# A four-layer graph network: an LSTM written with Tanh alone, and other ranks for the last units and blocks

## The chip, the cores and the metric

The kernel runs on one core of a Trainium2 chip. The core has a matrix engine (TensorE, "PE" in the profile; its weight loads are "PEld"), a vector engine (VectorE, "DVE"), an engine for activation functions and scaled copies (ScalarE, "ACT"), a general engine (GpSimd, "POOL") and a queue for transfers (SyncE, "SP"). Each works through its own instructions in order and waits on semaphores for the others. Matmul results go to PSUM, everything else lies in SBUF. The metric is device time in microseconds (us) from the first to the last instruction and the little that lies around it.

## The reference

The input x has 128 graphs of 64 nodes with 256 features, in float32. Four layers follow each other, each `x = layernorm(x + layer(x, adj))`.

- Layer 0: aggregation with the normalised adjacency, 256 to 512 features, batch norm, ReLU, back to 256, batch norm.
- Layer 1: a Chebyshev step (it needs the largest eigenvalue of adj), layer norm, attention with 4 heads (softmax, so Exp), layer norm, an MLP with Gelu, layer norm.
- Layer 2: two graph convolutions, and then four LSTMs in turn over windows of p = 1, 2, 3 and 4 nodes, where the last hidden state of a window replaces its last node:

```python
def step(carry, x_t):
    h, c = carry
    g = x_t @ Wih.T + h @ Whh.T + bias
    i, f, gg, o = jnp.split(g, 4, axis=-1)
    c = jax.nn.sigmoid(f) * c + jax.nn.sigmoid(i) * jnp.tanh(gg)
    h = jax.nn.sigmoid(o) * jnp.tanh(c)
    return ((h, c), None)
```

- Layer 3: graph attention: a product with W, scores, softmax over neighbours (Exp), the weighted sum, and two layer norms around it.

The change uses that sigmoid(z) = (tanh(z/2) + 1) / 2.

## The kernel before

The work is cut into 16 blocks of 8 graphs (512 rows of 256 features). Layer 0 runs as a stage of its own. Then a second call of `flow` lays out everything else. `flow` is a planner that runs while the program is built: each task is a generator that yields its steps with an engine, a planned duration and what it needs (`step(e, us, ps, sl, ..., at, tbl)`: PSUM tiles, SBUF slots, a time at which its inputs are due, the activation table). The planner always takes, of all running tasks, the step that could start first, and the instructions of all engines are issued in that order. A margin per engine (`MARGIN`, line 30; line 177) is added to the time at which a step's input is due before steps are compared, so that a step with a fresh input stands behind one whose input has long been there. Among equals the smaller rank wins. Nothing of this runs on the chip: there, each engine follows the order written.

Tasks come in streams with a width (how many run at once) and a rank (lines 1677 to 1690):

- `end` (rank 2, width 4): layer 3 for the blocks 12 to 15 in halves, 8 tasks of `last_block`
- `gcn` (rank 3, width 2): layer 2's graph convolutions and the LSTM with p = 1, by block
- `seq` (rank 4, width 6): the end of layer 0 and layer 1, by block
- `units` (rank 5, width 2): the LSTMs with p = 2, 3, 4 in 16 units, all but the last three
- the last three units (rank 1.5, width 1, "urgent", which means without margin): p = 4 for the third group of graphs, and for the fourth in two halves
- `last` (rank 6, width 4): layer 3 for the blocks 0 to 11.

An LSTM unit (`lstm`, line 1025) takes up to 512 windows. The first step has no h: it needs the gates i, g and o (lines 1055 for the products, 1067 for the activations), i times g on POOL (line 1086), Tanh of the cell (line 1094) and o times that on DVE (line 1102, or an `out_of` that writes the result into the state). Later steps of a large unit use a Strassen scheme with seven products in place of eight (line 1127 for the matmuls; stages 1 to 4 evict and combine on ACT and DVE, lines 1165 to 1195; activations at 1203 to 1207, i times g on POOL at 1220, the cell on DVE at 1228 and 1231, Tanh at 1236, h at 1243). The units with half the graphs use `plain_steps` (line 1250): products at 1264 and 1266, activations at 1269, i times g on POOL at 1280, the cell at 1282 and 1284, Tanh at 1286, h at 1296. Writing to the state is at lines 1357 (p = 1) and 1389.

A block of layer 3 (`last_block`, line 1456): x is fetched by SP, h is copied on ACT (1467), turned on PE (359), added (1478) and normed (lines 272 to 274 on DVE, 308 on POOL, 311 on DVE, 314 on ACT). Then it is turned again (353, copies at 1492 and 1494), multiplied by W (1507, 1517, 1519), scored (1527, 1531, 1532, 1536 to 1540), put through Exp (1544), divided (1546, 1547), turned (1553, 1555), multiplied (1563), added (1574), normed and stored. In layer 1 Exp is at line 854 and Gelu at line 928. Before an activation whose function isn't in the table that ACT holds, the program has a load of a table.

Of the kernel before, what the change touches and what calls it, by code (L numbers as in the profile page):

```python
# [26 lines left out]
BG = B // NG  # L27
EPS = 1e-5
LAG, LAG_T = 0.06, 0.2
MARGIN = {"T": 2.0, "V": 0.5, "S": 0.5}  # L30


@with_exitstack
def kernel(ctx: ExitStack, tc: tile.TileContext, a: dict, out: bass.AP):
# [23 lines left out]
    class Clock:  # L58
        end = 0.0
# [914 lines left out]
    bl = load_col(gw, "bih", a["L2_gnn_bih"])  # L974
    bh = load_col(gw, "bhh", a["L2_gnn_bhh"])
    V.tensor_tensor(bl, bl, bh, ALU.add)

    def gcn_rows():

# [45 lines left out]
    def lstm(p, n, parts, x_of, out_of):  # L1025

        us = n * 1.68e-3
        v_us, g_us, s_us = (0.05 + n * r for r in (1.25e-3, 2.3e-3, 1.15e-3))  # L1030

        def bias(g, c):
            return bl[:, p - 1, 2 * g + c : 2 * g + c + 1]

        def of(sl):
            return mem[sl][:, : 2 * n].rearrange("p (c k) -> p c k", c=2)
# [25 lines left out]
            return t, ps, sl  # L1062

        def gates(pair, t, ps, sl):
            t = yield step("S", 0.1 + n * 2.5e-3, ps=-1, at=t, waits=False, tbl="sigmoid")
            for j, (g, c) in enumerate(pair):
                S.activation(of(sl)[:, j], fm(PS[ps])[:, j, :n], AF.Tanh if g == 2 else AF.Sigmoid, bias=bias(g, c))  # L1067
            PS.give(ps)
            return t, sl

# [10 lines left out]
        for c in range(2):  # L1081
            if c:
                tb, sb = yield from gates(((0, 1), (2, 1)), *other)
            t, sl = (tb, sb) if c else (ta, sa)
            t = yield step("G", g_us, at=t, waits=False)
            G.tensor_tensor(of(s_cell)[:, c], of(sl)[:, 0], of(sl)[:, 1], ALU.mult)
            tc_.append(t)
        t_o, s_o = yield from gates(((3, 0), (3, 1)), *to)
        s_h = None
        for c in range(2):  # L1090
            sl = (sa, sb)[c]
            th = of(sl)[:, 1]
            t = yield step("S", s_us, at=tc_[c], waits=False, tbl="sigmoid")
            S.activation(th, of(s_cell)[:, c], AF.Tanh)
            o = of(s_o)[:, c]
            t = yield step("V", v_us, at=max(t, t_o), sl=0 if p == 1 or c else 1, waits=False)
            if p == 1:
                last_h(c, o, th)
            else:
                if c == 0:  # L1100
                    s_h = mem.take()
                V.tensor_tensor(of(s_h)[:, c], o, th, ALU.mult)
            mem.give(sl)
            h_at = t
        mem.give(s_o)

        if len(parts) == 1 and p > 1:
            yield from plain_steps(p, n, us, of, bias, x_of, lambda ap: spread(ap, 0), last_h, s_cell, s_h, h_at)
            return


# [24 lines left out]
        for s in range(1, p):  # L1136
# [59 lines left out]

            def stage4(g):
                v, y = places(g)
                f = AF.Tanh if g == 2 else AF.Sigmoid
                t = yield step("T", us, at=max(t_h[2], at[g]), waits=False)  # L1200
                product(g, "A22", T4, v[:, 0, :])
                yield step("S", 0.1 + n * 1.15e-3, at=at[g, "0"], waits=False, tbl="sigmoid")
                S.activation(of(act[g])[:, 0], of(act[g])[:, 0], f, bias=bias(g, 0))  # L1203
                yield step("S", copy_us, at=at[g], waits=False, tbl="sigmoid")
                S.activation(y[:, 3, :], y[:, 3, :], f, bias=bias(g, 1))
                at[g] = yield step("S", copy_us, ps=-1, at=t, waits=False, tbl="sigmoid")
                S.activation(y[:, 2, :], v[:, 0, :], f, bias=bias(g, 1))
                PS.give(tiles[g])

            yield from stage1(0)  # L1210
# [5 lines left out]
            yield from stage4(0)  # L1216
            yield from stage1(1)
            yield from stage4(2)
            t_g = yield step("G", 2 * g_us, at=at[2], waits=False)
            G.tensor_tensor(of(act[2]), of(act[0]), of(act[2]), ALU.mult)  # L1220
            mem.give(act[0])
            yield from stage1(3)
            for stage in (stage2, stage3):
# [1 line left out]
                yield from stage(3)  # L1225
            yield from stage4(1)
            yield step("V", 2 * v_us, at=at[1], waits=False)
            V.tensor_tensor(cell, cell, of(act[1]), ALU.mult)
            mem.give(act[1])
            t = yield step("V", 2 * v_us, at=t_g, waits=False)  # L1230
            V.tensor_tensor(cell, cell, of(act[2]), ALU.add)
            yield from stage4(3)
            for j in held:
                mem.give(j)
            t = yield step("S", 2 * s_us, at=t, waits=False, tbl="sigmoid")
            S.activation(of(act[2]), cell, AF.Tanh)
            t = yield step("V", 2 * v_us, at=max(t, at[3]), sl=0 if last else 1, waits=False)
            if last:
                for c in range(2):
                    last_h(c, of(act[3])[:, c], of(act[2])[:, c])  # L1240
            else:
                s_h = mem.take()
                V.tensor_tensor(of(s_h), of(act[3]), of(act[2]), ALU.mult)
# [6 lines left out]
    def plain_steps(p, n, us, of, bias, x_of, shaped, last_h, s_cell, s_h, h_at):  # L1250

        v_us, g_us, s_us = (0.05 + n * r for r in (1.25e-3, 2.3e-3, 1.15e-3))
        for s in range(1, p):
            last = s == p - 1
            x = x_of(s, 0)

            def products(pair):
                t = yield step("T", 8 * us, ps=1, sl=1, at=h_at - 2 * us, waits=False)
                ps, sl = PS.take(), mem.take()
                for j, (g, c) in enumerate(pair):  # L1260
                    m = slice(g * D + c * P, g * D + (c + 1) * P)
                    dst = fm(PS[ps])[:, j, :n]
# [4 lines left out]
                t = yield step("S", 0.3 + n * 2.1e-3, ps=-1, at=t, waits=False, tbl="sigmoid")  # L1267
                for j, (g, c) in enumerate(pair):
                    S.activation(of(sl)[:, j], fm(PS[ps])[:, j, :n], AF.Tanh if g == 2 else AF.Sigmoid, bias=bias(g, c))
                PS.give(ps)  # L1270
                return t, sl

            ends = []
            for c in range(2):
                cell = of(s_cell)[:, c]
                ta, sa = yield from products(((0, c), (2, c)))
                tb, sb = yield from products(((1, c), (3, c)))
                A, F = of(sa), of(sb)
                tg = yield step("G", g_us, at=ta, waits=False)
                G.tensor_tensor(A[:, 1], A[:, 0], A[:, 1], ALU.mult)  # L1280
                t = yield step("V", v_us, at=tb, waits=False)
                V.tensor_tensor(cell, cell, F[:, 0], ALU.mult)
                t = yield step("V", v_us, at=max(t, tg), waits=False)
                V.tensor_tensor(cell, cell, A[:, 1], ALU.add)
                t = yield step("S", s_us, at=t, waits=False, tbl="sigmoid")
                S.activation(A[:, 1], cell, AF.Tanh)
                ends.append((c, t, sa, sb))

            for c, t, sa, sb in ends:
                t = yield step("V", v_us, at=t, sl=0 if last or c else 1, waits=False)  # L1290
                if last:
                    last_h(c, of(sb)[:, 1], of(sa)[:, 1])
                else:
                    if c == 0:
                        h_new = mem.take()
                    V.tensor_tensor(of(h_new)[:, c], of(sb)[:, 1], of(sa)[:, 1], ALU.mult)
                mem.give(sa)
                mem.give(sb)
            mem.give(s_h)
            if not last:  # L1300
                s_h = h_new
            h_at = t
        yield step("V", 0.0, at=h_at, waits=False)
        mem.give(s_cell)

    def gcn_block(i):
# [47 lines left out]


        def out_of(q, c, o, th):
            V.tensor_tensor(
                hT_block(i)[:, c, :, :].rearrange("p n b -> p b n"), o, th, ALU.mult
            )

        yield step("T", 0.0)
# [6 lines left out]
    def unit(p, g, w0, nw, b0, nb):  # L1368
# [17 lines left out]
            return half(src[:, :, :, s, :], q)  # L1386

        def out_of(q, c, o, th):
            V.tensor_tensor(half(src[:, c, :, p - 1, :], q), o, th, ALU.mult)

        yield from lstm(p, nw * nb, parts, x_of, out_of)
        mark("p", p, g, w0, nw, b0, nb)
# [63 lines left out]
    def last_block(i, t0=0, nt=NT):  # L1456
# [18 lines left out]
        mem.give(s_h)  # L1475
        mark("read", i)
        yield step("V", 0.1 + 1.2 * r, ps=-1)
        V.tensor_tensor(x, px, x, ALU.add)
        PS.give(ps)
        yield from ln_steps_act(x)  # L1480

# [189 lines left out]
    def last_of(i, *part):  # L1671
# [67 lines left out]
```

## Time and profile before

| | us |
|---|---|
| median of 3 runs | 2408.22 (2407.28 to 2410.26) |
| profiled execution | 2409.44 |
| its span | 2407.7 |
| busy: PE / DVE / ACT / POOL | 2287.2 / 1287.7 / 1187.4 / 591.7 |
| mean granted PE clock | 0.982 |

The profile is of one execution. Busy times are sums over the span; the clock is a share of full speed. A line such as "L1086 POOL ... x12 | 15.3, 1276" names a line of the kernel, the engine, the operation, the count, the summed time in us and the mean time of one in ns; what follows is how long the engine stood idle before them and for whom it waited. The DVE line of the page, in 40 slices of the span, shows where that engine is busiest:

```profile
DVE  4557678566483474744643433454444444455546
ACT  2257643544434544335453443444444653468766
```

Layer 1 runs to about slice 20, the LSTM units from there to slice 37, layer 3 beside the last of them and after.

### The profile page before, as it was taken

The page shows a single profiled execution, that of the slowest core. Times are in us where ns is not written, and L with a number is a line of the kernel's source. Part 1 is how long each engine was busy: PE and PEld are TensorE (multiplying, and loading weights), DVE is VectorE, ACT ScalarE, POOL GpSimd, SP SyncE. Part 2 cuts the span into 40 slices and gives each one's busy share as a digit, 9 for nine tenths or more (in the row PEclk, how much of TensorE's full clock was granted, in tenths as well). Part 3 has the DMA queues.
Part 4 walks back from the last instruction along what each step waited for, and adds up shares of the span by engine and source line. Part 5 has one row for each costly group of instructions (what it writes and reads, how often), then busy time and mean ns, then how long its engine had stood idle before and what let it go on. Part 6 is the DMA issues. An engine that isn't in the chain of part 4 may idle for free.

```text
span 2407.7 us, 40603 instructions
## 1 busy us (share of the span) xinstructions
PE 2287.2 (95%) x16916; PEld 1759.9 (73%) x16916; DVE 1287.7 (53%) x2904; ACT 1187.4 (49%) x2189; POOL 591.7 (25%) x441
## 2 busy tenths in 40 slices
PE   8999788999989999999999999999999999998997
PEld 4548665666665666666667788899999888887785
DVE  4557678566483474744643433454444444455546
ACT  2257643544434544335453443444444653468766
POOL 0012134232242232331321222222221222122122
PEclk9999899999999999999999999999999999999998
DMA  6100301000000000001000000000001000001111
GB/s 162 49 1 1 111 23 49 28 10 10 1 12 17 10 10 10 1 10 36 36 19 27 18 1 1 17 2 1 1 1 36 1 10 9 19 27 66 40 36 45
DMA packets 42633, 57.91 MB, mean 24 GB/s; under 512 B 6224, under 2 KB 35536, under 8 KB 42448
## 3 DMA queue, kind: packets, MB, share of 16 engines
q1 hardware_dynamic: 41344, 54.22, 7.0%
q8 instruction: 133, 2.18, 0.4%
q10 hardware_dynamic: 1104, 1.08, 0.1%
q14 instruction: 52, 0.43, 0.1%
HBM read 38.52 MB, written 16.78 MB: 23 GB/s over the span
## 4 chain that ended last, share of the span: by engine, by line
PE 60%; DVE 16%; ACT 7%; POOL 3%; issue 2%; POOLq 0%; ACTq 0%; DVEq 0%
PE ps L1127 26%; PE ps L1055 11%; PE ps L365 7%; PE ps L377 4%; PE ps L938 4%; DVE ln_st L272 3%; ACT x L314 2%; PE ps L808 2%; POOL ln_rs L308 1%; PE ps L1507 1%; DVE x L300 1%; PE ps L341 1%; DVE ln_mv L273 1%; PE ps L353 1%; DVE ln_nm L311 1%
## 5 line engine op out<-in xcount | busy, mean ns | idle before, releaser
L1127 PE MATMUL ps<-x,x 128*128 128x256 f32 x928 | 225.0, 380 | 0.7 <-DVE t L1195 0.7
L1127 PEld LDWEIGHTS ps<-x,x 128*128 128x128 f32 x928 | 173.5, 190 | 24.9 <-issue 1.6
L314 ACT ACTIVATE x<-x,ln_nm,ln_rs 128x256 f32<-128x256 f32 x212 | 112.3, 592 | 133.3 <-DVE ln_nm L311 131.9
L1127 PE MATMUL ps<-t,x 128*128 128x256 f32 x672 | 163.7, 380 | 0.0
L1127 PEld LDWEIGHTS ps<-t,x 128*128 128x128 f32 x672 | 126.4, 190 | 17.1 <-DVE x L1195 0.8
L308 POOL TENSOR_TENSOR ln_rs<-ln_rs,neghalf 128x4 f32<-128x4 f32 (+1 forms) x72 | 71.2, 990 | 212.0 <-DVE ln_rs L274 186.4
L365 PE MATMUL ps<-t,W1T 128*128 128x512 f32 x256 | 117.8, 607 | 0.0
L1055 PE MATMUL ps<-h,wL 128*128 128x192 f32 (+2 forms) x480 | 103.9, 371 | 4.8 <-ACT h L1353 4.8
L272 DVE BATCH_NORM_STATS2 ln_st<-x 128x6 f32<-128x256 f32 x260 | 99.7, 403 | 0.4
L1055 PEld LDWEIGHTS ps<-h,wL 128*128 128x128 f32 x480 | 75.6, 192 | 29.9 <-issue 22.5
L294 POOL TENSOR_TENSOR ln_rs<-ln_rs,neghalf 128x4 f32<-128x4 f32 x32 | 36.9, 1153 | 217.1 <-DVE ln_rs L274 217.0
L1055 PE MATMUL ps<-h,x 128*128 128x256 f32 x384 | 86.7, 380 | 2.2 <-ACT t L1067 1.8
L1067 ACT ACTIVATE t<-ps,bih 128x512 f32<-128x512 f32 (+3 forms) x98 | 57.2, 634 | 55.8 <-PE ps L1055 55.1
L1203 ACT ACTIVATE x<-x,bih 128x512 f32<-128x512 f32 (+2 forms) x69 | 44.6, 648 | 80.3 <-DVE x L1193 80.0
L1186 DVE COPY x<-ps 128x256 f32<-128x256 f32 (+2 forms) x69 | 26.1, 378 | 108.4 <-PE ps L1127 107.6
L365 PEld LDWEIGHTS ps<-t,W1T 128*128 128x128 f32 x256 | 47.6, 195 | 49.6 <-issue 49.5
L365 PE MATMUL ps<-t,wA 128*128 128x512 f32 x160 | 76.8, 626 | 5.5 <-ACT t L784 5.5
L1055 PEld LDWEIGHTS ps<-h,x 128*128 128x128 f32 x384 | 72.6, 190 | 12.9 <-ACT t L1067 2.2
L1186 DVE COPY t<-ps 128x256 f32<-128x256 f32 (+2 forms) x51 | 18.8, 373 | 103.8 <-PE ps L1127 103.5
L1067 ACT ACTIVATE x<-ps,bih 128x512 f32<-128x512 f32 (+3 forms) x86 | 51.5, 650 | 40.6 <-PE ps L1055 40.4
L273 DVE BATCH_NORM_AGGREGATE ln_mv<-ln_st 128x2 f32<-128x6 f32 x448 | 71.3, 167 | 0.0
L1193 DVE TENSOR_TENSOR x<-ps,x 128x512 f32<-128x512 f32 (+2 forms) x69 | 41.4, 602 | 53.0 <-PE ps L1127 43.6
(714 smaller groups left out, 5713.2 us busy)
## 6 DMA issues: line engine op xcount, KB each, us to landing
t<-in_x_dram SPq DMA_DIRECT2D x26, 512.0 KB, 4.3
xd<-x SPq DMA_DIRECT2D x16, 512.0 KB, 2.6
x<-xd SPq DMA_DIRECT2D x8, 512.0 KB, 3.3
out_dram<-x SPq DMA_DIRECT2D x8, 512.0 KB, 2.9
h<-in_x_dram SPq DMA_DIRECT2D x5, 512.0 KB, 5.2
wL<-in_L_gnn_Wih_dram SPq DMA_DIRECT2D x2, 1024.0 KB, 5.0
x<-in_L_gnn_Whh_dram SPq DMA_DIRECT2D x2, 1024.0 KB, 5.4
x<-xd SPq DMA_DIRECT2D x5, 256.0 KB, 2.9
```

The source lines that it names most:

```text
L272: V.bn_stats(st[:, t, :], y[:, t, :])
L273: V.bn_aggr(mv[:, t, :], st[:, t, :])
L308: G.tensor_tensor(rs, rs, neghalf[:, :n], ALU.pow)
L314: S.activation(y[:, t, :], y[:, t, :], AF.Identity, scale=rs[:, t : t + 1], bias=nm[:, t : t + 1])
L365: T.matmul(ps[:, c, :], w[:, k, (off + c) * P : (off + c + 1) * P], yT[:, k, :], start=(k == 0), stop=(k == nk - 1),)
L377: T.matmul(ps[:, t, :], yT[:, k, t * P : (t + 1) * P], w[:, k, :], start=(k == 0), stop=(k == nk - 1),)
L808: T.matmul(pv[r * N : (r + 1) * N, b, :, :], x1T[:, k, b * N : (b + 1) * N], Wv_par[:, k, r, :, :], start=(k == 0), stop=(k == 1),)
L938: T.matmul(tm(PS[ps])[:, t, :], fm(mem[gs[k // 2]])[:, k % 2, t * P : (t + 1) * P], W2[:, k, :], start=(k == 0), stop=(k == 3),)
L1055: T.matmul(spread(fm(PS[ps])[:, j, :n], q), WL[p][0][:, k, m], x_of(0, q)[:, k], start=(k == 0), stop=(k == 1),)
L1067: S.activation(of(sl)[:, j], fm(PS[ps])[:, j, :n], AF.Tanh if g == 2 else AF.Sigmoid, bias=bias(g, c))
L1127: T.matmul(dst, WS[p][name](k, g), y[:, k], start=first and k == 0, stop=k == 1, skip_group_check=not first)
L1186: V.tensor_copy(y[:, 1, :], v[:, 0, :])
```

## The change

All gates use Tanh. A gate that was sigmoid(z) is now tanh(z/2), and what multiplies it adds one: (tanh(z/2) + 1) times y is twice sigmoid(z) times y. So the cell and h are kept doubled. A helper `gate` scales the product by 0.5 (0.25 for a sigmoid gate of a p above 1, whose inputs are doubled themselves), the biases of i, f and o are halved once, and layer 3 halves h when it adds it to x. Inputs of the LSTM with p = 1 aren't doubled.

i times g goes from POOL to DVE (`times`, a scalar_tensor_tensor). The planned steps of the LSTM no longer name an activation table.

In the planner, the margin for PE goes from 2.0 to 0.5, the last three units join the stream `units` (rank 5, width 2, with margin), and `end` goes from rank 2 to 5.5.

```diff
-MARGIN = {"T": 2.0, "V": 0.5, "S": 0.5}
+MARGIN = {"T": 0.5, "V": 0.5, "S": 0.5}
...
     V.tensor_tensor(bl, bl, bh, ALU.add)
+    for j in (slice(0, 4), slice(6, 8)):
+        V.tensor_scalar(bl[:, :, j], bl[:, :, j], 0.5, None, ALU.mult)
...
-        def bias(g, c):
-            return bl[:, p - 1, 2 * g + c : 2 * g + c + 1]
+        def gate(dst, z, g, c):
+            S.activation(
+                dst,
+                z,
+                AF.Tanh,
+                bias=bl[:, p - 1, 2 * g + c : 2 * g + c + 1],
+                scale=(1.0 if g == 2 else 0.5) * (1.0 if p == 1 else 0.5),
+            )
+
+        def times(dst, y, z):
+
+            V.scalar_tensor_tensor(dst, y, 1.0, z, ALU.add, ALU.mult)
...
-            t = yield step("S", 0.1 + n * 2.5e-3, ps=-1, at=t, waits=False, tbl="sigmoid")
+            t = yield step("S", 0.1 + n * 2.5e-3, ps=-1, at=t, waits=False)
             for j, (g, c) in enumerate(pair):
-                S.activation(of(sl)[:, j], fm(PS[ps])[:, j, :n], AF.Tanh if g == 2 else AF.Sigmoid, bias=bias(g, c))
+                gate(of(sl)[:, j], fm(PS[ps])[:, j, :n], g, c)
...
-            t = yield step("G", g_us, at=t, waits=False)
-            G.tensor_tensor(of(s_cell)[:, c], of(sl)[:, 0], of(sl)[:, 1], ALU.mult)
+            t = yield step("V", v_us, at=t, waits=False)
+            times(of(s_cell)[:, c], of(sl)[:, 0], of(sl)[:, 1])
...
-            S.activation(th, of(s_cell)[:, c], AF.Tanh)
+            t = yield step("S", s_us, at=tc_[c], waits=False)
+            S.activation(th, of(s_cell)[:, c], AF.Tanh, scale=0.5)
...
-                V.tensor_tensor(of(s_h)[:, c], o, th, ALU.mult)
+                times(of(s_h)[:, c], o, th)
...
-                S.activation(of(act[g])[:, 0], of(act[g])[:, 0], f, bias=bias(g, 0))
+                gate(of(act[g])[:, 0], of(act[g])[:, 0], g, 0)
...
-            t_g = yield step("G", 2 * g_us, at=at[2], waits=False)
-            G.tensor_tensor(of(act[2]), of(act[0]), of(act[2]), ALU.mult)
+            t_g = yield step("V", 2 * v_us, at=at[2], waits=False)
+            times(of(act[2]), of(act[0]), of(act[2]))
...
-            V.tensor_tensor(cell, cell, of(act[1]), ALU.mult)
+            times(cell, of(act[1]), cell)
...
-            V.tensor_tensor(cell, cell, of(act[2]), ALU.add)
+            V.scalar_tensor_tensor(cell, cell, 0.5, of(act[2]), ALU.mult, ALU.add)
...
-                G.tensor_tensor(A[:, 1], A[:, 0], A[:, 1], ALU.mult)
+                tg = yield step("V", v_us, at=ta, waits=False)
+                times(A[:, 1], A[:, 0], A[:, 1])
...
-            V.tensor_tensor(half(src[:, c, :, p - 1, :], q), o, th, ALU.mult)
+            V.scalar_tensor_tensor(half(src[:, c, :, p - 1, :], q), o, 1.0, th, ALU.add, ALU.mult)
...
-        V.tensor_tensor(x, px, x, ALU.add)
+        V.scalar_tensor_tensor(x, px, 0.5, x, ALU.mult, ALU.add)
...
-            Stream(4, 2, end),
+            Stream(4, 5.5, end),
             Stream(2, 3, gcn),
             Stream(6, 4, seq),
-            Stream(2, 5, units[:-3]),
-            Stream(1, 1.5, units[-3:], urgent=True),
+            Stream(2, 5, units),
             Stream(4, 6, last),
```

The remaining lines do the same at the other places of the LSTM (the Tanh of the cell, the later steps of both schemes, the write of p = 1).

More of the change, by code (lines that the diff above doesn't have):

```diff
@@ L1092, in lstm @@
             th = of(sl)[:, 1]
-            t = yield step("S", s_us, at=tc_[c], waits=False, tbl="sigmoid")
-            S.activation(th, of(s_cell)[:, c], AF.Tanh)
+            t = yield step("S", s_us, at=tc_[c], waits=False)
+            S.activation(th, of(s_cell)[:, c], AF.Tanh, scale=0.5)
             o = of(s_o)[:, c]
@@ L1107, in lstm @@
         if len(parts) == 1 and p > 1:
-            yield from plain_steps(p, n, us, of, bias, x_of, lambda ap: spread(ap, 0), last_h, s_cell, s_h, h_at)
+            yield from plain_steps(p, n, us, of, gate, times, x_of, lambda ap: spread(ap, 0), last_h, s_cell, s_h, h_at)
             return
@@ L1198, in stage4 @@
                 v, y = places(g)
-                f = AF.Tanh if g == 2 else AF.Sigmoid
                 t = yield step("T", us, at=max(t_h[2], at[g]), waits=False)
                 product(g, "A22", T4, v[:, 0, :])
[L1202 to L1207, printed above, removed]
+                yield step("S", 0.1 + n * 1.15e-3, at=at[g, "0"], waits=False)
+                gate(of(act[g])[:, 0], of(act[g])[:, 0], g, 0)
+                yield step("S", copy_us, at=at[g], waits=False)
+                gate(y[:, 3, :], y[:, 3, :], g, 1)
+                at[g] = yield step("S", copy_us, ps=-1, at=t, waits=False)
+                gate(y[:, 2, :], v[:, 0, :], g, 1)
                 PS.give(tiles[g])
@@ L1234, in lstm @@
                 mem.give(j)
-            t = yield step("S", 2 * s_us, at=t, waits=False, tbl="sigmoid")
-            S.activation(of(act[2]), cell, AF.Tanh)
+            t = yield step("S", 2 * s_us, at=t, waits=False)
+            S.activation(of(act[2]), cell, AF.Tanh, scale=0.5)
             t = yield step("V", 2 * v_us, at=max(t, at[3]), sl=0 if last else 1, waits=False)
@@ L1242, in lstm @@
                 s_h = mem.take()
-                V.tensor_tensor(of(s_h), of(act[3]), of(act[2]), ALU.mult)
+                times(of(s_h), of(act[3]), of(act[2]))
             mem.give(act[3])
@@ L1248, in lstm, with plain_steps @@
         mem.give(s_cell)
-    def plain_steps(p, n, us, of, bias, x_of, shaped, last_h, s_cell, s_h, h_at):
+    def plain_steps(p, n, us, of, gate, times, x_of, shaped, last_h, s_cell, s_h, h_at):
         v_us, g_us, s_us = (0.05 + n * r for r in (1.25e-3, 2.3e-3, 1.15e-3))
@@ L1266, in products @@
                         T.matmul(dst, WL[p][1][:, k, m], of(s_h)[:, k], start=False, stop=(k == 1))
-                t = yield step("S", 0.3 + n * 2.1e-3, ps=-1, at=t, waits=False, tbl="sigmoid")
+                t = yield step("S", 0.3 + n * 2.1e-3, ps=-1, at=t, waits=False)
                 for j, (g, c) in enumerate(pair):
-                    S.activation(of(sl)[:, j], fm(PS[ps])[:, j, :n], AF.Tanh if g == 2 else AF.Sigmoid, bias=bias(g, c))
+                    gate(of(sl)[:, j], fm(PS[ps])[:, j, :n], g, c)
                 PS.give(ps)
@@ L1278, in plain_steps @@
                 A, F = of(sa), of(sb)
-                tg = yield step("G", g_us, at=ta, waits=False)
-                G.tensor_tensor(A[:, 1], A[:, 0], A[:, 1], ALU.mult)
+                tg = yield step("V", v_us, at=ta, waits=False)
+                times(A[:, 1], A[:, 0], A[:, 1])
                 t = yield step("V", v_us, at=tb, waits=False)
-                V.tensor_tensor(cell, cell, F[:, 0], ALU.mult)
+                times(cell, F[:, 0], cell)
                 t = yield step("V", v_us, at=max(t, tg), waits=False)
-                V.tensor_tensor(cell, cell, A[:, 1], ALU.add)
-                t = yield step("S", s_us, at=t, waits=False, tbl="sigmoid")
-                S.activation(A[:, 1], cell, AF.Tanh)
+                V.scalar_tensor_tensor(cell, cell, 0.5, A[:, 1], ALU.mult, ALU.add)
+                t = yield step("S", s_us, at=t, waits=False)
+                S.activation(A[:, 1], cell, AF.Tanh, scale=0.5)
                 ends.append((c, t, sa, sb))
@@ L1295, in plain_steps @@
                         h_new = mem.take()
-                    V.tensor_tensor(of(h_new)[:, c], of(sb)[:, 1], of(sa)[:, 1], ALU.mult)
+                    times(of(h_new)[:, c], of(sb)[:, 1], of(sa)[:, 1])
                 mem.give(sa)
@@ L1356, in out_of @@
         def out_of(q, c, o, th):
-            V.tensor_tensor(
-                hT_block(i)[:, c, :, :].rearrange("p n b -> p b n"), o, th, ALU.mult
+            V.scalar_tensor_tensor(
+                hT_block(i)[:, c, :, :].rearrange("p n b -> p b n"), o, 1.0, th, ALU.add, ALU.mult
             )
```

## The prediction

> **What bounds the kernel now.** I read the page first, then one table by stage, then what holds TensorE up in the stages that lose time.
>
> ```profile
> PE 2287.2 (95%) x16916; PEld 1759.9 (73%) x16916; DVE 1287.7 (53%) x2904; ACT 1187.4 (49%) x2189; POOL 591.7 (25%) x441
> ...
> PEclk9999899999999999999999999999999999999998
> ```
>
> Matmuls fill 95% of the span; no other engine passes 53%. The change neither adds nor removes a matmul (8,844 in the program of either kernel), so it can only act on the 120.5 us in which TensorE stands still and on the slower clock after such gaps. Where these lie, from the windows view (length; then busy time of PE, PEld, DVE, ACT and POOL; then granted clock, DMA share, GB/s):
>
> ```profile
> 0.00:300.00 300.00, 266.51 (x2004) 178.37 (x2005) 174.33 (x363) 148.14 (x250) 31.01 (x41) 0.95 0.22 65
> 300.00:1260.00 960.00, 912.15 (x8578) 609.04 (x8577) 576.39 (x1246) 432.70 (x560) 306.98 (x186) 0.98 0.05 18
> 1260.00:2100.00 840.00, 834.57 (x4550) 743.09 (x4549) 369.67 (x719) 382.90 (x853) 188.61 (x136) 1.00 0.03 10
> 2100.00:2369.20 269.20, 252.09 (x1630) 213.31 (x1629) 144.84 (x477) 196.94 (x458) 56.62 (x66) 0.99 0.12 41
> 2369.20:2407.70 38.50, 21.84 (x161) 16.12 (x160) 22.50 (x101) 26.72 (x71) 8.53 (x14) 0.82 0.15 49
> ```
>
> PE idle by row: 33.5 (layer 0, before the first difference in the order), 47.9 (layer 1 and layer 2's graph part), 5.4 (the LSTM stage), 17.1 (the last LSTM units beside layer 3), 16.7 (the tail after the last LSTM matmul). The LSTM stage, which most of the edits touch, runs PE at 99.4%: nothing is to be had there. The other rows decide. What ACT does in them, by groups of instructions:
>
> ```profile
> L928 ACT ACT_TABLE_LOAD x18 | 23.1, 1283 | 3.2 <-issue 2.3 <-PE ps L365 0.6
> ...
> L1067 ACT ACT_TABLE_LOAD x17 | 21.8, 1283 | 33.9 <-PE ps L1055 33.7
> ...
> L1544 ACT ACT_TABLE_LOAD x16 | 20.5, 1283 | 5.5 <-DVE mx L1540 5.3
> ...
> L854 ACT ACT_TABLE_LOAD x13 | 16.7, 1283 | 13.3 <-DVE h L852 9.5 <-DVE t L852 3.6
> ```
>
> With fifteen more (ten at line 1269, five at lines 1203, 1205 and 584) there are 79 loads, 1.28 us each, because Sigmoid, Exp and Gelu sit in different tables. On the chain of waits (start, length, what) between 2150 and 2300 thirteen of them stand, for example:
>
> ```profile
> 2158.49 1.28 ACT L1544
> ...
> 2161.24 1.28 ACT L1203
> ```
>
> PE's own waits from 2100 on are spread over many small ones, behind ACT, DVE and POOL alike:
>
> ```profile
> PE ps L353 <- ACT x L314: 2.9, 1, 2.9
> PE ps L1563 <- ACT h L1555: 2.8, 1, 2.8
> PE ps L1553 <- ACT t L1207: 2.5, 1, 2.5
> ```
>
> [...] The order of the changed kernel agrees: 19 loads are left, eight for Exp and nine for Gelu in layer 1, one at line 584 and one for Exp later; none stands at an LSTM line, so Tanh also runs from the table that Gelu loaded. [...] at 2161.24 the load begins 20 ns after the instruction before it ended, and the next starts 10 ns after the load. I use 1.28. [...] line 1228 on 128x768 takes 0.95 us in most instances and 2.56 in one, line 1231 on 128x1024 takes 1.22 in most groups and 1.55 on average in another. [...] in the tail row above the clock is 0.82.
>
> **The change part by part.**
>
> *Tanh for Sigmoid.* The activations keep number and shape; a constant factor in place of none is not shown as a price of its own, and I take zero. 60 loads go: 60 x 1.283 = 77 us less ACT work. Beside a full PE most of this is worth nothing. On the path it can return what stood on the chain: 13 x 1.28 = 16.7 us at 2150 to 2300, and four loads (at 480.9, 489.7, 1140.4 and 1225.0) = 5.1 us in layers 1 and 2. It can't return more than PE was idle (17.1 us in the fourth row), and once a load is gone the next wait is a layer norm's (DVE statistics, POOL power, ACT scaling). I take 11 and 4; bounds 3 to 17 and 0 to 20 (the upper end if the 40 us of loads freed in layers 1 and 2 also shorten other blocks' chains).
>
> *Products with "+1" on DVE.* 119 multiplications leave POOL (lines 1086, 1220, 1280: 87 + 67 + 9 = 163 us) and come to DVE as scalar_tensor_tensor. Row by row such an instruction costs what a tensor_tensor does (line 1538: 420 ns, line 1547: 423 ns, both 128x256), so DVE gains 74 x about 0.6 + 33 x about 1.05 + 12 x 0.42 = 84 us, mostly in the LSTM stage, where it is 44% busy. A link of the chain falls from 1.27 to 0.69 us (128x512), under a full PE: zero. Queued behind them on DVE are the evictions of the Strassen products; 84 us in 840 more raise DVE to 54%, which I price at zero to +3. With 163 us less of POOL [...] I take -2 (bounds -6 to 0). The halved biases are two small instructions (line 274's kind, 0.26 us each) beside layer 1: zero. Line 1478's addition becomes one that also halves, at the same price.
>
> *Ranks and streams.* The last three LSTM units join the common stream of two, and layer 3's last half blocks fall behind the LSTM. In the changed order 6.5 of layer 3's 16 blocks end after the last LSTM matmul (four whole ones and five halves); before it was 2.5. So the tail grows and what lies before it shrinks. A whole block costs PE, from the timeline at full clock, 0.87 + 0.87 (transposes) + 3.65 (Wx) + 0.86 (scores) + 0.6 + 1.03 = 7.9 us. What is issued after the last LSTM matmul sums to 48 us of PE (17 before), 60 of ACT (before: 26.7 by the same count, and the window shows 26.72), 63 of DVE (28 by the same count, where the window shows 22.5 because short instructions overlap, so about 50). ACT decides. Between 2160 and 2220 ACT reached 90%, in the old tail 69%. At 85% the tail takes 60/0.85 + 4 for the last copies and store = 74 us. Of it 26 are not PE work; in the old tail 38.5 - 17 = 21.5 were not. Cost: +4; bounds -4 (95%) to +15 (69%).
> The order of SP's loads moves with it: x of blocks 14 and 15 is fetched late, behind a store that waits for its block, yet 2.6 us per fetch lie beside 4 us of that block's own copies: zero to +3.
>
> *PE margin 2.0 to 0.5.* It changes the order nearly everywhere from layer 1 on: a product may now be placed when its input is due 0.5 us ahead instead of 2. Against that, older blocks go first and free their buffers. The number of changes from task to task on PE is the same (999 and 998). The trace can't price this. From below: -12, a quarter of the 47.9 us. From above: PE waited about 30 times in layers 1 and 2, some 1.6 us each; half as many again with a slower clock after some is +25. I take zero.
>
> Sum: -11 - 4 - 2 + 4 = -13. The profiled execution took 2409.4 (span 2407.7), so 2396.4; the median shown is 1.2 below that execution, so 2395.2. I say 2396.
>
> **The rivals.**
> 1. The tail decides (slower). Layer 3's last blocks are the only work left, each a chain of ACT, DVE, POOL and PE. If ACT reaches only 60% of it, the tail takes about 100 us, 52 of them not PE work: +30. Less 17 of gains: 2422. It decides from a tail of 48 + 21.5 + 17 = 87 us on. For it: the old tail reached 69% with few blocks. Against: eight blocks may run at once now.
> 2. The margin's stalls eat the gain: +16 in layers 1 and 2, 2412. For it: PE's waits are many and short. Against: in the LSTM stage, where products follow each other densely, PE waits 5 us in 840.
> 3. More comes back in layers 1 and 2: of 47.9 us idle and 2% of clock over 960 us (19 us) a third returns, 22 in place of 4: 2378.
> 4. The loads were covered and layer norm holds PE as before: the gains shrink to about 4, the tail takes 4: 2409.
>
> **How the numbers follow.** Forecast 0.40 (own range 2384 to 2406), rival 1 0.18, rival 2 0.17, rival 3 0.15, rival 4 0.10. Within 0.2% (what a measurement can tell from no change) is 2403.4 to 2413.0. Faster: 0.85 of the forecast, rival 3, a tenth of rival 2: 0.51. Same: 0.12 of the forecast, 0.6 of rival 4, 0.35 of rival 2: 0.17. Slower: 0.32. Eight times in ten: 2375 to 2424.
>
> **What would show it.** In the new profile: 19 loads, ACT near 1110 us, DVE near 1370, POOL near 430, PE unchanged near 2287 and 99% busy in the LSTM stage. From the last LSTM matmul to the end 65 to 84 us, ACT its busiest engine; PE idle before that below 8 us over a stretch like the old fourth row; PE idle from 300 to 1260 near 44. I am wrong if the tail exceeds 87 us, if the idle time in layers 1 and 2 grows by 10 us or more, or if the LSTM stage falls below 98%.

## The result and the profile after

The changed kernel takes 2440.07 us (median of four runs, 2439.28 to 2441.58), against 2407.75 us for the kernel before on the same chip: a ratio of 1.0133 with a 95% interval of 1.0115 to 1.0150. It is 1.3% slower, where the prediction said 0.5% faster. The profiled execution has a span of 2437.5 us, 29.8 more than before.

The head of the page after (busy time and share of the span by engine, number of instructions, and the granted clock in 40 slices):

```profile
PE 2294.5 (94%) x16916; PEld 1768.3 (73%) x16916; DVE 1325.7 (54%) x3025; ACT 1113.4 (46%) x2129; POOL 431.7 (18%) x322
...
PEclk9999899999989999999999999999999999999997
```

The matmuls are the same 16916 records, yet they took 7.3 us longer; the other engines moved as their instructions did. The loss has to lie in the time in which TensorE stood still and in its clock, so the windows view is read next. Its columns are length; busy time of PE, PEld, DVE, ACT, POOL; granted clock, DMA share, GB/s. The fourth row ends with the last LSTM matmul, as it did in the prediction.

```profile
0.00:300.00 300.00, 266.18 (x2005) 178.36 (x2006) 174.89 (x365) 148.36 (x250) 31.32 (x41) 0.95 0.23 65
300.00:1260.00 960.00, 891.78 (x8338) 599.65 (x8337) 559.09 (x1254) 383.78 (x515) 259.57 (x151) 0.97 0.05 17
1260.00:2080.00 820.00, 812.09 (x4636) 716.27 (x4636) 400.40 (x796) 381.22 (x847) 90.45 (x72) 1.00 0.03 12
2080.00:2350.10 270.10, 264.13 (x1511) 228.86 (x1510) 136.68 (x389) 144.03 (x363) 31.53 (x34) 0.99 0.09 29
2350.10:2437.50 87.40, 60.30 (x433) 45.14 (x431) 54.65 (x226) 55.98 (x156) 18.82 (x25) 0.81 0.15 49
```

Length less PE's busy time is the time that TensorE stood still. Against the same stages before:

| stage | idle before | idle after | |
|---|---|---|---|
| layer 0 (0 to 300) | 33.5 | 33.8 | +0.3 |
| layers 1 and 2 (300 to 1260) | 47.9 | 68.2 | +20.3 |
| LSTM (1260 to 2080) | 5.4 | 7.9 | +2.5 |
| to the last LSTM matmul | 17.1 | 6.0 | -11.1 |
| tail | 16.7 | 27.1 | +10.4 |
| PE busy over all | 2287.2 | 2294.5 | +7.3 |

The tail grew from 38.5 to 87.4 us, and that is what the eye falls on. But the long tail holds 60.3 us of PE work, where the old one held 21.8. Its idle time grew by 10.4, and that of the stage before shrank by 11.1: together nothing. The loss is layers 1 and 2, and the slower clock. Who PE waited for there, from the view of waits between 300 and 1260 us (in total, times, longest):

```profile
PE ps L341 <- ACT t L1343: 6.3, 1, 6.3
PE ps L938 <- ACT x L928: 6.1, 1, 6.1
PE ps L1071 <- ACT t L1368: 5.7, 1, 5.7
PE ps L365 <- ACT t L784: 5.5, 1, 5.5
PE ps L938 <- DVE t L898: 5.5, 1, 5.5
```

Two of these, the fourth and fifth, are there before as well. The first three are new, and each is one long stall. In this stretch after has eight single stalls of 3.3 us or more, 40 us together, where before has five, 24 us: 16 of the 20.3 us are long stalls. The third can be followed through the timeline of after (start, length, engine, line, operation, count, and in brackets the idle time before it):

```profile
524.65 0.46 DVE L297 SCALAR_TENSOR_TENSOR h<-h,ln_mv,rows 128x256 f32<-128x256 f32 x1
...
526.86 0.88 DVE L300 SCALAR_TENSOR_TENSOR h<-h,ln_rs,rows 128x256 f32<-128x256 f32 x2
527.66 5.07 DVE L297 SCALAR_TENSOR_TENSOR h<-h,ln_mv,rows 128x256 f32<-128x256 f32 x2
...
536.54 2.33 DVE L274 TENSOR_SCALAR ln_rs<-ln_mv 128x4 f32<-128x4 f32 x1
...
542.14 1.28 DVE L1360 TENSOR_TENSOR t<-ps,rb 128x512 f32<-128x512 f32 x2
...
527.40 2.55 POOL L915 TENSOR_TENSOR h<-h,rows 128x1024 f32<-128x1024 f32 x1 [0.58 <-PE ps L353]
530.03 2.41 POOL L916 TENSOR_TENSOR h<-h,rows 128x1024 f32<-128x1024 f32 x1
...
536.23 2.61 POOL L933 TENSOR_TENSOR x<-x,rows 128x1024 f32<-128x1024 f32 x1 [3.79 <-DVE h L776]
...
543.52 1.06 ACT L1368 ACTIVATE t<-t 128x1024 f32<-128x1024 f32 x1 [13.81 <-DVE t L1360]
...
535.31 3.62 PE L377 MATMUL ps<-wA,t 128*128 128x256 f32 x16
544.62 13.38 PE L1071 MATMUL ps<-t,wL 128*128 128x512 f32 x24 [5.70 <-ACT t L1368]
...
713.16 2.29 DVE L311 SCALAR_TENSOR_TENSOR ln_nm<-ln_mv,ln_rs 128x4 f32<-128x4 f32 x1 [1.12 <-POOL ln_rs L308]
...
713.10 2.34 POOL L915 TENSOR_TENSOR t<-t,rows 128x1024 f32<-128x1024 f32 x1
715.49 2.07 ACT L314 ACTIVATE x<-x,ln_nm,ln_rs 128x256 f32<-128x256 f32 x4 [11.11 <-DVE ln_nm L311]
...
719.70 1.05 ACT L1343 ACTIVATE t<-t 128x1024 f32<-128x1024 f32 x1
```

One DVE instruction of line 297 takes 0.46 us, and the next two take 5.07 together, beside two of POOL's. Line 274, 0.26 us on average before, takes 2.33 beside POOL's third. That is 4.15 + 2.07 = 6.2 us of delay, which the DVE queue hands on to line 1360, from there to the Relu on ACT at 1368, and so to the product at 1071 behind which PE's whole queue stands. Over the whole trace of after 62 DVE instructions took at least 0.5 us more than the median of their line and shape, and each of the 62 overlaps an instruction of POOL; in before it is 90 of 90. But 503 of the 3025 DVE instructions of after overlap one, so that most of these keep their time. Lines 297 and 311 read two tensors, line 274 reads one, and all three have stretched instances; what sets the stretched ones apart, the traces don't show.

The last four lines belong to the 6.3 us stall. DVE's small line 311 takes as long as POOL's line 915 beside it, some 2 us more than its usual 0.16. ACT's line 314 waits for it, and behind 314 in ACT's queue stands line 1343, for which PE waits. So the stretched instruction accounts for some 2 of the 6.3 us, and the rest is work that was queued ahead. The 6.1 us stall has no such pair: ACT's line 928 stands behind line 314, which had waited 13.12 us for a layer norm.

Such stretched instructions are not new in the changed kernel. Line 285, another part of a layer norm, has them before (first line) and after (second; count, then shortest, median and longest in ns):

```profile
L285 DVE TENSOR_SCALAR t<-t,ln_mv,ln_rs x40: 375/408/2532, 352.2 to 1224.6; 128x256 f32<-128x256 f32 x40
L285 DVE TENSOR_SCALAR t<-t,ln_mv,ln_rs x36: 374/407/2428, 354.8 to 1187.1; 128x256 f32<-128x256 f32 x36
```

Counted over all DVE instructions that took at least 0.5 us more than the median of their line and shape, the excess in layers 1 and 2 is 87 us before and 62 after. There is less of it, then, and yet PE stood still for longer: the amount of stretching doesn't explain the loss.

Such a stall costs twice. The 24 products behind this one took 13.38 us. The same 24, with no stall ahead of them, in the timeline of before:

```profile
551.18 10.46 PE L1055 MATMUL ps<-t,wL 128*128 128x512 f32 x24
```

The windows view of after shows the clock behind the stall (the 0.50 and the 1.00):

```profile
543.60:550.30 6.70, 5.67 (x7) 2.52 (x8) 5.73 (x16) 2.13 (x3) 3.47 (x2) 0.50 0.01 2
550.40:557.90 7.50, 7.50 (x19) 3.29 (x18) 5.62 (x8) 3.16 (x5) 2.34 (x1) 1.00 0.00 0
```

PE worked for 5.67 us at half its clock, and half of that, 2.8 us, is nearly all of the 2.9 us that the products took longer. So a stall of 5.7 us cost 2.9 more in the work that followed. It is not alone in this: in the trace of after PE stands still for 4.2 us or more between two matmuls 11 times, and in the 2 us behind each of these stalls the clock is 0.50.

### The profile page after: what moved, and what is told of

It is laid out like the page before. It is cut to its first block, busy times and chain, and to the rows that moved or that the text cites. A ratio compares the mean times of both kernels' runs of the same rounds, so it can differ in the third digit from the quotient of the medians.

```text
span 2437.5 us, 40485 instructions
## 1 busy us (share of the span) xinstructions
PE 2294.5 (94%) x16916; PEld 1768.3 (73%) x16916; DVE 1325.7 (54%) x3025; ACT 1113.4 (46%) x2129; POOL 431.7 (18%) x322
## 4 chain that ended last, share of the span: by engine, by line
PE 50%; DVE 11%; ACT 4%; issue 2%; POOL 1%; POOLq 0%; ACTq 0%; DVEq 0%
PE ps L1143 24%; PE ps L1071 10%; PE ps L365 5%; PE ps L938 2%; DVE ln_st L272 2%; PE ps L1522 2%; PE ps L377 2%; PE ps L1279 1%; PE ps L1281 1%; DVE x L300 1%; POOL ln_rs L308 1%; ACT t L1039 1%; ACT x L314 1%; PE ps L808 1%; PE ps L341 1%
## 5 line engine op out<-in xcount | busy, mean ns | idle before, releaser
L1039 ACT ACTIVATE x<-ps,bih 128x512 f32<-128x512 f32 (+5 forms) x182 | 94.9, 560 | 108.4 <-PE ps L1071 68.1
L1143 PE MATMUL ps<-t,x 128*128 128x256 f32 x576 | 142.2, 380 | 0.1
L1039 ACT ACTIVATE t<-ps,bih 128x512 f32<-128x512 f32 (+5 forms) x176 | 90.9, 552 | 97.9 <-PE ps L1071 75.4
L1143 PEld LDWEIGHTS ps<-t,x 128*128 128x128 f32 x576 | 107.7, 190 | 16.3 <-issue 2.4
L1039 ACT ACTIVATE t<-t,bih 128x512 f32<-128x512 f32 (+5 forms) x128 | 66.5, 556 | 80.6 <-DVE t L1209 76.7
L1071 PE MATMUL ps<-h,wL 128*128 128x192 f32 (+2 forms) x456 | 90.5, 352 | 0.0
L272 DVE BATCH_NORM_STATS2 ln_st<-x 128x6 f32<-128x256 f32 x228 | 87.0, 402 | 0.2
L1039 ACT ACTIVATE x<-x,bih 128x512 f32<-128x512 f32 (+2 forms) x108 | 56.0, 551 | 56.6 <-DVE x L1209 53.5
L1071 PE MATMUL ps<-x,wL 128*128 128x512 f32 x168 | 73.3, 593 | 0.7 <-ACT x L1368 0.7
L1071 PE MATMUL ps<-t,wL 128*128 128x512 f32 x144 | 65.8, 615 | 5.7 <-ACT t L1368 5.7
```

The source lines that it names most:

```text
L272: V.bn_stats(st[:, t, :], y[:, t, :])
L1039: S.activation(dst, z, AF.Tanh, bias=bl[:, p - 1, 2 * g + c : 2 * g + c + 1], scale=(1.0 if g == 2 else 0.5) * (1.0 if p == 1 else 0.5),)
L1071: T.matmul(spread(fm(PS[ps])[:, j, :n], q), WL[p][0][:, k, m], x_of(0, q)[:, k], start=(k == 0), stop=(k == 1),)
L1143: T.matmul(dst, WS[p][name](k, g), y[:, k], start=first and k == 0, stop=k == 1, skip_group_check=not first)
```

## The experiments

All ratios are against the kernel before, measured beside each (2407.7 to 2408.4 us). "Idle" is PE's idle time between 300 and 1260 us of the profiled execution.

### The parts apart

The change has three parts: the arithmetic (Tanh, doubled state, products on DVE, loads gone), the ranks and streams, and the margin.

**tanh_old_order**: the arithmetic alone. The planner is told the old steps, margin and streams, so that TensorE follows almost the order of before: of the 16916 records 34 stand at another line. Some of its edits (the others give the remaining LSTM steps their old engine or table):

```diff
-MARGIN = {"T": 0.5, "V": 0.5, "S": 0.5}
+MARGIN = {"T": 2.0, "V": 0.5, "S": 0.5}
...
-            t = yield step("V", v_us, at=t, waits=False)
+            t = yield step("G", g_us, at=t, waits=False)
             times(of(s_cell)[:, c], of(sl)[:, 0], of(sl)[:, 1])
...
-            Stream(4, 5.5, end),
+            Stream(4, 2, end),
...
-            Stream(2, 5, units),
+            Stream(2, 5, units[:-3]),
+            Stream(1, 1.5, units[-3:], urgent=True),
```

> The arithmetic of the changed kernel (Tanh gates, products on DVE) under the planned steps, margin and streams of the kernel before, so that TensorE's order is nearly that of before. Theory A (the arithmetic is a small gain, the order is the loss): 2390 to 2404 us, fewer table loads, PE idle from 2100 on 5 to 12 us less. Theory B (84 us more work on DVE holds up the evictions in the LSTM stage): 2415 us or more, with PE idle growing between 1260 and 2100. Theory C (the loads were covered and nothing comes back): 2404 to 2412.

Measured: 2391.34 us, 0.9932 (0.9918 to 0.9947): 16.4 us faster, with 23 loads left. The view of windows of this kernel:

```profile
300.00:1260.00 960.00, 915.57 (x8601) 611.76 (x8602) 584.60 (x1284) 404.83 (x543) 270.00 (x156) 0.98 0.05 18
2080.00:2350.20 270.20, 261.08 (x1690) 224.38 (x1688) 151.86 (x504) 163.55 (x438) 37.85 (x44) 0.99 0.12 41
2350.20:2390.40 40.20, 22.77 (x161) 17.05 (x160) 22.80 (x102) 26.07 (x70) 9.06 (x15) 0.80 0.14 47
```

PE's idle time fell by 3.5 us in layers 1 and 2 (to 44.4) and by 8.0 beside layer 3 (to 9.1); the tail stayed. This is the one comparison here in which the order is nearly fixed, so that what differs is the instructions.

**tanh_only**, **margin_back**, **streams_back** and **margin_alone** put single parts of the two plans together. The edits are the lines on the margin and on the streams above, each alone: tanh_only is the changed kernel with the old margin and streams, margin_back with the old margin, streams_back with the old streams; margin_alone is the kernel before with the margin at 0.5.

> The changed kernel with margin 2.0 and the old streams; only the LSTM's planned steps are those of the changed kernel, so the order is drawn anew. A: 2390 to 2408. B: 2415 or more. If the new draw of the order alone is worth as much as the other edits, it lies 10 us or more from the run with the old order.

> The changed kernel with PE's margin at 2.0 again, new ranks and streams kept. If the margin made the 20 us more idle time in layers 1 and 2: 2415 to 2424, PE idle from 300 to 1260 back near 48. If the margin is innocent: 2435 to 2445.

> The changed kernel with the old ranks and streams, margin 0.5 kept. If the ranks made the long tail (87 us against 38): the tail is back near 40 us, and the time 2405 to 2425. If the tail only pays back what the stretch before it gained: 2430 to 2442. PE idle from 300 to 1260 stays near 68 either way if the margin made it.

> The kernel before with PE's margin at 0.5 and nothing else. If the margin costs by itself, whatever the arithmetic: 2435 to 2460 us, PE idle from 300 to 1260 above 62. If it only costs together with the Tanh LSTM: 2403 to 2415.

| arithmetic, streams | margin 2.0 | margin 0.5 | difference |
|---|---|---|---|
| old, old | before, 2407.8 (idle 47.9) | margin_alone, 2462.84 (78.2) | +55 |
| new, old | tanh_only, 2402.66 (43.9) | streams_back, 2451.07 (65.8) | +48 |
| new, new | margin_back, 2403.71 (45.0) | after, 2440.07 (68.2) | +36 |

The ratios are 1.0228 (1.0213 to 1.0243) for margin_alone, 0.9983 (0.9974 to 0.9991) for tanh_only, 1.0180 (1.0165 to 1.0195) for streams_back and 0.9979 (0.9972 to 0.9986) for margin_back. In all three pairs the short margin costs, also where nothing else is changed. The streams cost 1 us at the old margin and gain 11 at the new one. tanh_only differs from tanh_old_order only in what the planner is told of the LSTM's steps, and is 11.3 us slower. So one way through the parts is: arithmetic -16.4, its planned steps +11.3, streams +1.0, margin +36.4, together +32.3. Each of these but the first is the difference of two orders; how far a single order can be trusted is the last question below. Three results lie outside every range that was expected: margin_back 11 us below, streams_back 9 and margin_alone 3 above. The rows of margin_back:

```profile
300.00:1260.00 960.00, 915.01 (x8403) 618.67 (x8404) 573.83 (x1282) 403.51 (x549) 264.90 (x152) 0.98 0.05 17
2080.00:2331.10 251.10, 245.60 (x1386) 211.24 (x1385) 125.89 (x368) 134.97 (x338) 29.20 (x33) 0.99 0.09 29
2331.10:2400.70 69.60, 43.75 (x353) 32.62 (x351) 40.81 (x169) 41.75 (x127) 13.10 (x19) 0.85 0.15 50
```

Its tail is 18 us shorter than that of after, but idles 25.8 us against 27.1. Of the 36.8 us between the two spans 23.2 are idle time in layers 1 and 2, and 16.6 are PE's busy time (2277.9 against 2294.5); what is left is -3.0.

### How much margin

**margin_1** and **margin_3h** are the changed kernel with 1.0 and 3.5, **old_order_3h** is tanh_old_order with 3.5. The edit of margin_1:

```diff
-MARGIN = {"T": 0.5, "V": 0.5, "S": 0.5}
+MARGIN = {"T": 1.0, "V": 0.5, "S": 0.5}
```

> The changed kernel with PE's margin at 1.0. If the cost falls steadily with the margin: 2415 to 2432, between 2440 (0.5) and 2404 (2.0). If the order at 0.5 is one bad draw: within 6 us of 2404, or anywhere.

> The changed kernel with PE's margin at 3.5. If more cover is better: 2390 to 2403. If 2.0 already covers the lateness and a larger margin only delays the blocks that others wait for: 2403 to 2415.

> The fastest order so far (Tanh arithmetic, planned steps, ranks and streams of the kernel before) with margin 3.5 in place of 2.0. If the margin's gain adds to it: 2378 to 2388. If the order at 2.0 was a lucky draw: 2388 to 2402.

| margin | 0.5 | 1.0 | 2.0 | 3.5 |
|---|---|---|---|---|
| time | 2440.07 | 2410.54 | 2403.71 | 2394.30 |
| idle | 68.2 | 52.5 | 45.0 | 39.7 |

margin_1 is at 1.0010 (1.0004 to 1.0017), margin_3h at 0.9944 (0.9927 to 0.9961), old_order_3h at 0.9908 (0.9891 to 0.9924), that is 2385.99 us with an idle time of 27.9. Time and idle time fall together in this row of four. The step from 0.5 to 1.0 is the largest, 29.5 us, and puts margin_1 below the 2415 to 2432 of a steady fall. But all three steps lie within what the last group of experiments shows to be the scatter of single orders, so that the form of the row isn't shown.

### Is it late inputs, and where

**lag_up** leaves the margin at 0.5 and lets the planner add more to the end of every planned step, which puts dependent work further behind on all engines. **lag_and_margin** has both. The edit of lag_up:

```diff
-LAG, LAG_T = 0.06, 0.2
+LAG, LAG_T = 0.5, 0.6
```

> The changed kernel, margin 0.5 kept, but the planner adds 0.5 us (0.6 after PE) to every step's end before the next step of the task is due, in place of 0.06 and 0.2. Theory L (inputs come later on the chip than planned, and 0.5 us of margin doesn't cover it): most of the 36 us comes back, 2400 to 2418. Theory P (a small margin always prefers the oldest block, so that too few blocks are under way, whatever the delays): 2430 to 2445.

> The changed kernel with both covers: 0.5 and 0.6 us after each planned step, and margin 2.0. If cover for late inputs still lacks at margin 2.0: 2385 to 2398. If either alone is enough: 2396 to 2405.

lag_up took 2400.79 us, 0.9971 (0.9961 to 0.9981), idle 46.9: as fast as with the old margin, as it would be if inputs come later than planned. lag_and_margin took 2426.91, 1.0075 (1.0060 to 1.0090), idle 63.2, and contradicts that: it has both covers and loses 23 us against margin_back. Its loss lies where layer 1 hands over to the LSTM units:

```profile
1100.00:1300.00 200.00, 175.42 (x1325) 123.11 (x1324) 99.07 (x199) 72.00 (x106) 41.06 (x23) 0.93 0.04 15
```

That is 24.6 us of idle time in 200, with the clock at 0.93; the kernel before has 6.3 and a clock of 1.00 there.

**margin_front** and **margin_rear** give the old margin to a part of the streams only: the first to ranks of 5 and more (LSTM units and layer 3), the second to ranks 3 and 4 (layers 1 and 2). The edit of margin_rear:

```diff
-                soon = max(t if r[6].urgent else t + margin.get(e, 0.0), free[e])
+                late = 2.0 if e == "T" and r[6].prio in (3, 4) else margin.get(e, 0.0)
+                soon = max(t if r[6].urgent else t + late, free[e])
```

> The changed kernel with PE's margin at 0.5 for layers 0 to 2's blocks (ranks 0 to 4) and 2.0 for the LSTM units and layer 3 (ranks from 5 on). If the cost arises in the blocks of layers 1 and 2: 2428 to 2445, PE idle from 300 to 1260 near 68. If it arises among units and layer 3: 2400 to 2412.

> The other half: margin 2.0 for the blocks of layer 1 and the graph part of layer 2 (ranks 3 and 4), 0.5 elsewhere. If the blocks carry the cost: 2400 to 2412, PE idle from 300 to 1260 near 45, although the LSTM stage keeps the small margin. If not: 2428 to 2445.

2432.70 us, 1.0100 (1.0085 to 1.0115), and 2442.10, 1.0139 (1.0124 to 1.0154). Neither half brings the gain back. margin_rear has the idle time up to 780 of margin_back (29.6 against 28.6) and loses it again between 780 and 1260 (35.8 against 16.4). So these two runs don't put the loss down to one set of streams; as each is a single order, they don't rule it out either.

### How much is the luck of one order

These misses raise a question: a tiny edit sends the planner another way, and every order is one draw. So the two margins were compared in other orders, each made by a small edit: the DVE margin 0.4 in place of 0.5 (**draw_m05_v**, **draw_m20_v**), LAG 0.08 in place of 0.06 (**draw_m05_lag**, **draw_m20_lag**), and lag_up and lag_and_margin again with 0.4 and 0.5 (**draw_late_m05**, **draw_late_m20**). The edit of draw_m20_v:

```diff
-MARGIN = {"T": 0.5, "V": 0.5, "S": 0.5}
+MARGIN = {"T": 2.0, "V": 0.4, "S": 0.5}
```

> The changed kernel (PE margin 0.5) with DVE's margin at 0.4 in place of 0.5: nearly the same rules, another order. If the margin of 0.5 is the cause: 2425 to 2455. If the order of the changed kernel was one bad draw: anywhere from 2395 to 2445.

> PE margin 2.0, new ranks, DVE's margin at 0.4. Margin as the cause: 2392 to 2412. If draws scatter by more than the margin is worth: above 2420 is as likely as below.

> The changed kernel (PE margin 0.5) with 0.08 in place of 0.06 us after a planned step: another order under nearly the same rules. Margin as the cause: 2425 to 2455; one bad draw: anywhere from 2395 to 2445.

> PE margin 2.0, new ranks, 0.08 in place of 0.06 us after a planned step. Margin as the cause: 2392 to 2412. If draws scatter by more than the margin is worth: above 2420 is as likely as below.

> The changed kernel with the planner's delays of a finished step at 0.4 and 0.5 us in place of 0.06 and 0.2 (the 0.5 and 0.6 of lag_up, a little less), PE margin 0.5. Theory L (what costs is that the PE is placed behind inputs that come later on the chip than planned; a longer delay per step hides that as a longer margin does): the gain of lag_up comes again, 2390 to 2412, PE idle between 300 and 1260 of at most 52 us. Theory D (each planned order is a draw, and lag_up's was a lucky one): anything from 2412 to 2440, with the idle above 55 us.

> The same delays of 0.4 and 0.5 us, with the PE margin at 2.0: lag_and_margin a second time with slightly shorter delays. If too much cover in itself costs (the PE is given so much slack that it lacks work at the hand-over from layer 1 to the LSTM units), 2415 to 2435 with some 20 us or more of PE idle between 1100 and 1300. If lag_and_margin's 2426.9 was the scatter of one planned order, 2370 to 2412, with at most 12 us of idle there.

| order | margin 0.5 | idle | margin 2.0 | idle | difference |
|---|---|---|---|---|---|
| as in the change | 2440.07 | 68.2 | 2403.71 | 45.0 | +36 |
| DVE margin 0.4 | 2438.12 | 64.8 | 2367.45 | 35.8 | +71 |
| LAG 0.08 | 2420.10 | 55.3 | 2407.06 | 54.4 | +13 |
| LAG 0.4, 0.5 | 2429.09 | 58.5 | 2387.59 | 45.0 | +42 |
| LAG 0.5, 0.6 | 2400.79 | 46.9 | 2426.91 | 63.2 | -26 |

The ratios of the new ones, from the top, first at 0.5 and then at 2.0: 1.0121 (1.0092 to 1.0151) and 0.9828 (0.9799 to 0.9856); 1.0044 (1.0024 to 1.0064) and 0.9996 (0.9986 to 1.0006); 1.0096 (1.0079 to 1.0113) and 0.9917 (0.9902 to 0.9932). Both results on LAG fell with the last pair: with 0.4 and 0.5 the short margin is slow again and the long one fast. So lag_up looks like a lucky order and lag_and_margin like an unlucky one, and neither says anything of cover as such. draw_m05_lag and draw_m20_v lie below the ranges that were given for the margin as the cause, by 5 and 25 us.

The first three orders, which differ by tiny edits, spread over 20 us (0.5) and 40 us (2.0); all five over 39 and 59. The two pairs with the old streams added, the seven differences have a mean of 34 us and a standard deviation of 32: 34 +- 30 at 95%, if the orders are taken as random ones. Six of seven have the same sign. The five pairs of the table alone give 27 +- 45, which does not exclude zero. What speaks more plainly is where the single orders lie: of the seven with a margin of 0.5 everywhere six took 2420 us or more, and of the eleven with 1.0 or more only one did. The margin matters, then, but what it is worth in a given order can't be told beforehand to better than some tens of us.

What goes with the time is TensorE's idle time in the trace. Over the profiles of all 20 kernels, each with 16916 matmul records, idle time in layers 1 and 2 and span go together with a correlation of 0.95, lucky or not: below 46 us of idle time every span is under 2401, above 60 every one is over 2424. A us more of it goes with 1.8 us of span, 0.65 of which is PE's busy time. The stretched DVE instructions don't go with it: their excess in layers 1 and 2 is 62 us in the best order, in margin_back and in after alike, and 65 in margin_alone. The best order, draw_m20_v (2366.07 to 2368.83 in two runs), beats both kernels. Its rows in the windows view:

```profile
300.00:1260.00 960.00, 924.19 (x8683) 624.37 (x8682) 575.46 (x1286) 406.50 (x547) 270.66 (x156) 0.99 0.05 18
1100.00:1300.00 200.00, 197.17 (x1440) 136.93 (x1439) 92.79 (x199) 84.81 (x129) 35.78 (x22) 1.00 0.06 22
2080.00:2311.50 231.50, 230.42 (x1331) 198.18 (x1330) 123.08 (x372) 128.99 (x330) 27.84 (x31) 1.00 0.10 33
2311.50:2364.30 52.80, 34.02 (x284) 24.46 (x283) 34.49 (x150) 36.69 (x110) 12.78 (x18) 0.88 0.18 61
```

The hand-over that cost lag_and_margin 24.6 us costs 2.8 here, the stretch before the tail 1.1, and 8683 records fit into the 960 us in which after had 8338.

## Why the prediction was wrong, point by point

- **Loads and products (-17): right with the order held.** The sum had -11, -4 and -2. tanh_old_order gives -16.4, with 8.0 us less idle time beside layer 3 and 3.5 less in layers 1 and 2. That the planner would also lay out the new LSTM steps differently was given no price; it came to +11.3 in the one pair of orders that tests it (5.2 more idle time in the LSTM stage, 6.8 more in the tail), which is within the scatter of orders. Without the margin the change gives -4 (margin_back) where -13 was the sum. 19 loads were left, as foretold: of the 666 gate activations in the trace of after (Tanh) 412 run with a load for Gelu as the last one before them and 254 with one for Exp; ACT (1113.4) and POOL (431.7) came as said.
- **DVE near 1370: 1325.7, though its new work was priced well.** Summed over instructions, the lines that changed took 310 us in place of 231, 79 more where 84 was said. What the prediction left out is that the other lines took 35 us less: line 285 alone, with 64 instructions in both kernels, took 30.6 us in place of 46.4, because fewer of them were stretched to some 2.4 us. POOL does 160 us less work, and every stretched instruction lies beside one of POOL's (90 of 90 before, 62 of 62 after). With the order held the stretched time over the whole span falls from 123 to 98 us (tanh_old_order). That the work gone from POOL is the reason was not tried alone, and the -2 that the prediction took for it stays an estimate without a measured price. As DVE isn't the bound, the miss cost nothing.
- **Ranks and streams (+4): neither confirmed nor refuted.** The tail is 87.4 us where 74 was said and 65 to 84 was the range. Of it 27.1 us are idle time, and 26 was said. But the old tail was read wrongly: 17 us of PE work were taken by a count of what is issued after the last LSTM matmul, so that 21.5 were left, while the windows view in the prediction shows 21.84 us of work and so 16.7 of idle time. By one measure for both tails the estimate was +9, and +10.4 was measured. The stage before gave 11.1 back (the 17.1 us, of which the loads had been given 11). Parted from the rest by margin_back against tanh_only, the streams cost 1 us, and at the short margin they gain 11; both are single pairs of orders, within their scatter. ACT being the busiest engine of the tail was wrong: it has 56.0 us, DVE 54.7 and PE 60.3. ACT reached 64% of it, near the 60% of rival 1.
- **"I am wrong if the tail exceeds 87 us": a false test.** It did, and the prediction was wrong, yet not by the tail. Tail length counts PE work that is due anyway; only its idle time is a cost. Rival 1 (2422) lies nearer to the result than the forecast, but its reason does not hold. The sign beside it, idle time in layers 1 and 2 growing by 10 us or more, was the right one: it grew by 20.3.
- **The PE margin ("I take zero", -12 to +25): the step that failed.** It cost 36 us against margin_back, above the upper bound, and 34 +- 30 over the seven pairs of orders. Idle time in layers 1 and 2 grew by 20.3 us against before and by 23.2 against margin_back, about the half of 47.9 that the upper bound had. What came with it was sized too small: PE's busy time rose by 16.6 us against margin_back, where the bound left 1 for the slower clock and the forecast had PE unchanged. In after PE worked 91 us at half clock, in margin_back 62; half of the difference, 14 us, is most of the 16.6. Rival 2 had the mechanism and half its size (+16).
- **Its argument failed too.** Rival 2 was held small since PE waits only 5 us in 840 in the LSTM stage. That stage still runs at 99.0%. The dense stage says nothing of layers 1 and 2, where chains through DVE, POOL and ACT feed PE and single stalls reach 6.3 us.
- **The range (2375 to 2424)** took one order's cost as known once its parts were. Tiny edits spread the orders of one margin over 20 and 40 us, and other settings of LAG over 39 and 59; where the order changes, a sum of parts can't be held to less than that. How much of this order's 36 us is the margin and how much the luck of the order, the runs don't tell.

What stays open: that late inputs come from DVE instructions stretched beside POOL is read from the trace of after for one stall and a part of a second, and was not tried alone; since kernels with much less idle time have as much of this stretching, it can't be the difference between the orders by itself. Nor is it shown that a longer margin helps by covering lateness, since the runs with LAG contradict each other. Why orders of one margin differ by up to 59 us is told only as far as where PE stood still.

## What to carry to other kernels

Where a planner writes the order of all engines, do not price a cut in the slack ahead of the engine that bounds the kernel at zero: here the shorter slack was slower in six of seven pairs of orders. Look first at how far single instructions stray from the times that the plan gives them (here a 0.26 us instruction took 2.33). A change of a planner's numbers is a draw: judge it over several equivalent orders, test arithmetic with the order held fixed, and when one order must be shipped, measure several and take the fastest; the bounding engine's idle time by stage says where the others lose. Do not price a stage by its length but by the time in which the bounding engine stands still in it.

## What the hardware showed unexpectedly

The same 16916 matmul records took between 2267.0 us (draw_m20_v) and 2303.4 us (margin_alone) of PE's time. Most of these 36 us is the granted clock: PE worked 44 us at half clock in the first and 107 in the second, and half of the difference is 32 us. The busy time follows the idle time in layers 1 and 2 with a correlation of 0.90. So on this engine the busy time is no constant of the work: a stall of 5.7 us made the 24 matmuls behind it take 13.38 us in place of 10.46. Whether long stalls cost more than the same idle time in short ones was not tried.
